# Features dealt in pairs, four more tiles turned by VectorE, and a new order of the whole program

## The chip, the cores and the metric

The kernel runs on one core of a Trainium2 chip. The metric is the device time of one execution in microseconds (us); less is better. Of TensorE (PE), VectorE (DVE), ScalarE (ACT), GpSimd (POOL) and SyncE (SP), the first four compute and SP issues the DMA transfers.

## The reference

x has 4 rows of 1024 positions with 512 features, the condition 256 features for each row, W 1536 x 512. For each row, relu of (x, the mean of x over the positions, the condition twice) times W plus b is added to x. All is float32:

```python
hidden = jnp.concatenate([cond_512, cond_512], axis=-1)
x_mean = jnp.mean(x, axis=1, keepdims=True)
fused = jnp.concatenate([x, x_mean * ones_L, hidden[:, None, :] * ones_L], axis=-1)
relation = jax.nn.relu(jnp.einsum('bld,do->blo', fused, W) + b)
return x + relation
```

The mean and the condition are the same at every position of a row, so their part of the product is one bias vector per row.

## The kernel before

The 4096 positions are cut into 32 tiles of 128 positions; a tile is multiplied by the first 512 rows of W. TensorE wants the features on the partitions, so every tile has to be turned first. The 512 features are dealt to four groups j = 0 to 3 of 128 features: feature 4a + j stands on partition a of group j. W is loaded to match (line 120).

Both x and W are split into a high part (rounded to the multiplier's format) and a low part (the rest). The task `h` makes x's high part on ScalarE, and sums over the positions beside it; `l` makes the low part on VectorE or GpSimd; `wh` and `wl` do the same for W. A tile and a group take three products on TensorE (line 348): high by high, low by high, high by low. That is 12 products of 128x512 for each tile, or 24 of half the width for the last one, t = 31, which is finished in two halves.

Tiles are turned in two ways, by units (`UNITS`). Units 0 to 3 (tiles 0; 1; 2 and 3; 4 to 7) are turned by TensorE: a 128x128 transpose for each tile and group that reads every fourth float of x's rows (task `T`, line 244). The others, four tiles each, are loaded a second time as `z` in 512-byte pieces, one DMA for each block of 32 partitions (task `Z`, four for each unit, three buffers), and VectorE turns 32x32 blocks of them (`T`, line 246), into PSUM for j = 0 and 2 and into SBUF for j = 1 and 3:

```python
zs[z_of(u)][:, : n * NQ].rearrange("p n (a j) -> p n j a", j=J)[:, :, j]
```

The bias of a row comes from the sums (`to`), W's second part (`M`, `m`, line 302), the third part and the condition (`V`, `ac`, `g`, `d`), a fold, a product with ones (`pb`, line 326) and a copy (`bc`). Products go to five PSUM banks. Tiles 0 to 11 (way K) are copied out (`K`), get the bias (`b`, GpSimd, line 419), a relu (`r`, ScalarE, line 427) and are added to x (`F`, GpSimd, line 431). Tiles 12 to 17 (way B) get the bias while they are copied out. The rest (way I) find the bias in the bank (`P`) and one VectorE operation does relu and addition (`F`, line 406). `S` stores a tile. `X` loads x for TensorE's turning and for the final addition; the x of tiles 4 to 7 stays in SBUF from the start to their addition.

Nothing is scheduled when the program is built: `ORDER`, a list of task names, is walked once, and each engine and SP's DMA queue get their instructions in that order. `@d`, `@a` and `@p` name the engine where a task has a choice. Each engine works its list in order. `fill` is a product on zeros that nobody reads.

Of the kernel before, what the change touches and what calls it, by code (L numbers as in the profile page):

```python
# [27 lines left out]
p1.3.2 l2.3@d p0.3.2 l2.2@d p1.2.1 T3.1 T3.3 h3.1 T3.0 ac0@p T3.2 K0@a l3.1@d Z5.0 Z5.1 p2.3 h3.0 t0 h3.3 p2.1
ac1@p g0.0 l3.3@d p3.0 l3.0@d d0.0 p1.3.1 p3.3 Z6.2 Z6.3 K1@a p2.2 h3.2 p5.0 g0.1 l3.2@d g1.0 p3.1 d0.1 T4.0
Z6.0 Z6.1 p6.1 T4.3 p6.3 d1.0 as0 h4.0 p4.1 T4.1 to0 p3.2 g2.0 m0.0 p2.0 K3@a m0.1 p5.2 h4.3 T4.2 p4.3 g1.1  # L30
h4.1 p5.1 d1.1 m0.2 Z7.0 Z7.1 K2@a p5.3 m0.3 h4.2 Z7.2 Z7.3 p6.0 l4.3@p l4.0@d f0 p7.3 l4.2@d g2.1 l4.1@p p6.2
fa0 p4.2 vh0 d2.0 K5@a T5.1 p4.0 p8.2 vl0 h5.1 p7.1 T5.3 K6@a l5.1@p p8.1 T5.0 h5.3 p8.0 d2.1 K4@a pb0 T5.2
# [20 lines left out]
def kernel(  # L53
# [123 lines left out]
    for part, (j0, n) in enumerate([(0, 2), (2, 2)]):  # L177
        @task(f"W{part}")
        def _(e, j0=j0, n=n):
            dma(e, out=xs[W_SLOT][:, j0 : j0 + n], in_=Wv[0, :, j0 : j0 + n])  # L180
    for h in range(2):
        @task("M" + "ab"[h])
        def _(e, h=h):
            dma(e, out=w_mean[:, 2 * h : 2 * h + 2], in_=Wv[1, :, 2 * h : 2 * h + 2])
# [38 lines left out]

    for u, (t0, n) in enumerate(UNITS):
        r = t0 // NK
        s = row_units[r].index(u)
        for j in range(J):
            buf, col = place[u, j]
            m = n * P
            if n == 1:  # L230
                xT = ps_x[u % 2][:, j * m : (j + 1) * m]
            elif n == 2:
                xT = (ps_o[4], acc)[j // 2][:, j % 2 * m : (j % 2 + 1) * m]
            elif u in BY_PE:
                xT = (*ps_x, ps_o[4], acc)[j]
# [234 lines left out]
```

## Time and profile before

| | us |
|---|---|
| median of 3 runs | 104.17 |
| lowest and highest | 103.57, 104.91 |
| span of the profiled execution (the only time that its page gives) | 104.4 |
| PE busy | 97.5 |
| DVE, ACT, POOL busy | 71.4, 62.2, 71.8 |

The span runs from the first to the last instruction of the profiled execution. A busy share is an average over the span; what a stage is worth is read from that stage's rows. In a row of instructions the first number is the start from the span's beginning, the second the length, and the brackets tell how long the engine was idle before it and what ended that. Matmuls overlap, so the distance between their starts, not their length, is what one costs. "px", "po" and "acc" are PSUM banks, "z" and "x" the two loads of x.

### The profile page before, as it was taken

The numbers are of one execution on the slowest core, as the hardware profiler recorded it, in microseconds if no ns is written. First come the engines' busy times: TensorE is split into PE (matmuls) and PEld (weight loads), VectorE is DVE, ScalarE is ACT, GpSimd is POOL, SyncE is SP. The second block draws the span as 40 slices with busy tenths as digits, with TensorE's granted clock in tenths as the row PEclk, the third lists the DMA queues.
The fourth block names the chain that finished last, engine by engine and source line by source line (L and its number), as shares of the span: only waits on it lengthen the run. The fifth ranks groups of instructions, "written<-read, shape, count | busy, mean of one in ns | idle before, by whom it ended". The sixth has DMA issues, their size and how long they took to land.

```text
span 104.4 us, 1435 instructions
## 1 busy us (share of the span) xinstructions
PE 97.5 (93%) x441; PEld 77.9 (75%) x441; DVE 71.4 (68%) x111; ACT 62.2 (60%) x154; POOL 71.8 (69%) x72
## 2 busy tenths in 40 slices
PE   6959999999978899999999999999999999999980
PEld 2347898888846588888888887887878888888870
DVE  1094946292899999999999999998968400622060
ACT  5248447879157785789984796899449502313000
POOL 4060609892970989996989999959999899904000
PEclk9999999999999999999999999999999999999999
...
GB/s 53 308 350 383 419 251 216 318 213 193 195 215 212 192 164 217 233 223 313 163 15 221 324 279 398 404 205 232 150 0 230 371 209 218 385 402 400 396 297 116
DMA packets 22657, 26.31 MB, mean 252 GB/s; under 512 B 1269, under 2 KB 13817, under 8 KB 22650
## 3 DMA queue, kind: packets, MB, share of 16 engines
...
q8 instruction: 3, 0.05, 0.2%
q14 instruction: 4, 0.03, 0.1%
...
## 4 chain that ended last, share of the span: by engine, by line
PE 77%; DVE 8%; DMA 6%; ACT 4%; issue 1%; POOL 1%; SPq 1%; POOLq 0%; DVEq 0%
PE po L348 73%; DMA x<-in_x_dram 6%; DVE acc L302 2%; DVE xT L246 2%; ACT hi L252 2%; ACT o L415 2%; PE acc L244 1%; DVE px L246 1%; PE po L244 1%; PE px L244 1%; PE acc L326 1%; DVE lo L258 1%; DVE v_acc L322 1%; DVE acc L314 1%; ACT term L280 1%
## 5 line engine op out<-in xcount | busy, mean ns | idle before, releaser
L348 PE MATMUL po<-w_hi,lo 128*128 128x512 f32 (+1 forms) x132 | 50.8, 386 | 1.2 <-DVE lo L258 1.2
L348 PE MATMUL po<-w_hi,hi 128*128 128x512 f32 (+1 forms) x132 | 50.8, 387 | 1.0 <-ACT w_hi L215 0.7
L348 PE MATMUL po<-w_lo,hi 128*128 128x512 f32 (+1 forms) x132 | 50.1, 385 | 0.0
L348 PEld LDWEIGHTS po<-w_hi,hi 128*128 128x128 f32 x132 | 24.8, 188 | 6.9 <-ACT w_hi L215 1.2
L348 PEld LDWEIGHTS po<-w_hi,lo 128*128 128x128 f32 x132 | 24.9, 188 | 6.3 <-DVE lo L258 1.6
L348 PEld LDWEIGHTS po<-w_lo,hi 128*128 128x128 f32 x132 | 24.8, 188 | 4.8
L431 POOL TENSOR_TENSOR x<-o,x 128x512 f32<-128x512 f32 x18 | 23.0, 1295 | 4.6 <-ACT o L427 4.6
L406 DVE SCALAR_TENSOR_TENSOR x<-po,x 128x512 f32<-128x512 f32 x13 | 8.8, 688 | 15.5 <-PE po L348 12.1
L258 POOL TENSOR_TENSOR lo<-xT,hi 128x512 fp32r<-128x512 f32 x12 | 15.5, 1297 | 3.7 <-ACT hi L252 3.6
L252 ACT ACTIVATE hi<-px 128x512 fp32r<-128x512 f32 (+1 forms) x22 | 10.4, 477 | 10.0 <-PE px L244 6.6
L258 DVE TENSOR_TENSOR lo<-px,hi 128x512 fp32r<-128x512 f32 (+1 forms) x22 | 11.4, 539 | 6.8 <-ACT hi L252 6.7
L419 POOL TENSOR_TENSOR o<-o,bias 128x512 f32<-128x512 f32 x12 | 15.3, 1294 | 0.0
L302 DVE SCALAR_TENSOR_TENSOR acc<-w_mean,tot,acc 128x512 f32<-128x512 f32 x16 | 11.9, 746 | 3.0 <-ACT o L415 2.5
L246 DVE STREAM_TRANSPOSE px<-z 128x512 f32<-128x512 f32 x12 | 13.0, 1100 | 0.9 <-DMA z<-in_x_dram 0.9
L427 ACT ACTIVATE o<-o 128x512 f32<-128x512 f32 x18 | 10.6, 620 | 4.9 <-POOL o L419 4.9
L246 DVE STREAM_TRANSPOSE xT<-z 128x512 f32<-128x512 f32 x12 | 13.0, 1086 | 0.0
L402 ACT ACTIVATE po<-bias 128x512 f32<-128x512 f32 x13 | 7.6, 592 | 3.5 <-DVE x L406 2.2
L252 ACT ACTIVATE hi<-xT 128x512 fp32r<-128x512 f32 x12 | 7.5, 624 | 1.2 <-DVE xT L246 1.2
L221 POOL TENSOR_TENSOR w_lo<-x,w_hi 128x256 fp32r<-128x256 f32 (+1 forms) x3 | 3.2, 1080 | 7.2 <-DVE w_hi L217 3.8
L415 ACT ACTIVATE o<-po 128x512 f32<-128x512 f32 x12 | 6.9, 586 | 0.8 <-PE po L348 0.8
L284 POOL TENSOR_TENSOR cond<-cond,term 128x512 f32<-128x512 f32 x4 | 5.2, 1293 | 2.6 <-ACT term L280 2.6
L280 ACT ACTIVATE term<-wc,cT 128x512 f32<-128x512 f32 x8 | 5.6, 715 | 0.4 <-POOL wc L274 0.4
...
## 6 DMA issues: line engine op xcount, KB each, us to landing
...
x<-in_L_cond_W_dram SPq DMA_DIRECT2D x1, 1024.0 KB, 10.6
w_mean<-in_L_cond_W_dram SPq DMA_DIRECT2D x2, 512.0 KB, 10.2
...
```

The lines of the kernel that those rows point to most:

```text
L246: nc.vector.transpose(xT.rearrange("p (n t) -> p n t", t=Q), zs[z_of(u)][:, : n * NQ].rearrange("p n (a j) -> p n j a", j=J)[:, :, j])
L252: nc.scalar.activation(his[buf][:, col : col + m], xT, AF.Copy, accum_out=sums[:, r, j, s : s + 1])
L258: nc_of[e].tensor_tensor(los[buf][:, col : col + m], xT, his[buf][:, col : col + m].bitcast(F32), ALU.subtract)
L280: nc.scalar.activation(terms[k], wc[:, k], AF.Copy, scale=cT[:, k, r : r + 1])
L302: nc.vector.scalar_tensor_tensor(acc, w_mean[:, j, :], tot[:, r, j : j + 1], acc, ALU.mult, ALU.add)
L348: nc.tensor.matmul(v, lhsT=a[:, col : col + P], rhs=m, start=WAYS[t] != "I" and key not in done, stop=done.count(key) == 3 * J - 1, skip_g ...
L402: nc.scalar.activation(bank(t), biases[r], AF.Copy)
L406: nc.vector.scalar_tensor_tensor(x_tile(t), bank(t), 0.0, x_tile(t), ALU.max, ALU.add)
L415: nc.scalar.activation(o, bank(t), AF.Copy)
L419: nc_of[e].tensor_tensor(o, o, biases[r], ALU.add)
L427: nc.scalar.activation(o, o, AF.Relu)
L431: nc.gpsimd.tensor_tensor(x_tile(t), o, x_tile(t), ALU.add)
```

## The change

Features are dealt otherwise: feature 8a + 2j + e stands on partition 2a + e of group j, so a group has pairs of neighbouring features. W's first two parts are loaded for even and odd partitions apart, in rows of 2 KB: `W` in three pieces for each parity, `M` in one. VectorE's transposes read pairs of floats, 32 bytes from pair to pair, where they read single floats 16 bytes apart.

Tiles 4 to 7 leave TensorE: they become the first unit that comes through z. For tiles 0 to 3 a copy (task `y`) gathers a group's 128 features side by side, and TensorE's transposes read that; the copies use the last four of the twelve parking buffers, and the banks that these transposes write are dealt anew. The relu of a parked tile may run on VectorE, and its addition to x on VectorE or GpSimd. `ORDER` is a new list.

```diff
-    UNITS = [(0, 1), (1, 1), (2, 2), (4, 4)] + [(t, 4) for t in range(NK, NT, 4)]
-    BY_PE = (0, 1, 2, 3)
+    E = 2
+    UNITS = [(0, 1), (1, 1), (2, 2)] + [(t, 4) for t in range(4, NT, 4)]
+    BY_PE = (0, 1, 2)
+    Y_PARTS = {0: [(0, 1), (1, 1), (2, 2)], 1: [(0, 2), (2, 2)]}
+    W_PARTS = [(0, 1), (1, 1), (2, 2)]
...
-    Wv = W.rearrange("(s p j) o -> s p j o", p=P, j=J)
+    Wv = W.rearrange("(s a j e) o -> s j a e o", s=3, j=J, e=E)
...
+    for i in range(E):
+        for part, (j0, n) in enumerate(W_PARTS):
+            @task(f"W{part}.{i}")
+            def _(e, i=i, j0=j0, n=n):
+                dma(e, out=xs[W_SLOT][i::E, j0 : j0 + n], in_=Wv[0, j0 : j0 + n, :, i].rearrange("j a o -> a j o"))
+
+        @task(f"M{i}")
+        def _(e, i=i):
+            dma(e, out=w_mean[i::E], in_=Wv[1, :, :, i].rearrange("j a o -> a j o"))
...
+    def gathered(t):
+        return parks[PARKS - 1 - t]
+
+    for t in range(sum(UNITS[u][1] for u in BY_PE)):
+        for h, (j0, n) in enumerate(Y_PARTS.get(t, [(0, J)])):
+            @task(f"y{t}.{h}")
+            def _(e, t=t, j0=j0, n=n):
+                dst = gathered(t).rearrange("p (j a e) -> p j a e", j=J, e=E)[:, j0 : j0 + n]
+                src = x_tile(t).rearrange("p (a j e) -> p j a e", j=J, e=E)[:, j0 : j0 + n]
+                if e == "a":
+                    nc.scalar.activation(dst, src, AF.Copy)
+                else:
+                    nc_of[e].tensor_copy(dst, src)
...
-                        v = x_tile(t0 + i).rearrange("p (f j) -> p j f", j=J)[:, j]
+                        v = gathered(t0 + i)[:, j * P : (j + 1) * P]
...
-                    xT.rearrange("p (n t) -> p n t", t=Q), zs[z_of(u)][:, : n * NQ].rearrange("p n (a j) -> p n j a", j=J)[:, :, j]
+                    xT.rearrange("p (n t) -> p n t", t=Q),
+                    zs[z_of(u)][:, : n * NQ].rearrange("p n (a j e) -> p n j a e", j=J, e=E)[:, :, j],
...
-            nc.scalar.activation(o, o, AF.Relu)
+            if e == "d":
+                nc.vector.tensor_scalar(o, o, 0.0, None, ALU.max)
+            else:
+                nc.scalar.activation(o, o, AF.Relu)
...
-            nc.gpsimd.tensor_tensor(x_tile(t), o, x_tile(t), ALU.add)
+            if e == "g":
+                nc.vector.scalar_tensor_tensor(x_tile(t), o, 0.0, x_tile(t), ALU.max, ALU.add)
+            else:
+                nc_of[e].tensor_tensor(x_tile(t), o, x_tile(t), ALU.add)
...
-relu X0.0 W0 B X0.1 X0.2 C W1 fill fill fill fill fill fill T0.2 T0.3 X1.1 T0.0 T0.1 X1.0 h0.0 V h0.1 l0.0@d
+X0.1 X0.0 fill relu W1.0 fill W1.1 fill W0.1 fill W0.0 fill W2.1 fill y1.1@d y1.0@p W2.0 fill X0.2 y0.2@d y0.0@p
```

TensorE's list before, from its third product on, so behind tile 0's four transposes, nine fills and two products (x_65 holds x of tiles 0 to 3, po_136 and po_137 the products of tiles 0 and 1, hi_75 and lo_89 tile 0's parts, hi_76 tile 1's high part; the rows at L244 are transposes):

```order
L348 MATMUL po_136<-w_hi,hi_75 128x512
L244 MATMUL px_142<-term_123,x_65 128x128 x4
L348 MATMUL po_136<-w_hi,lo_89 128x512
L348 MATMUL po_136<-w_lo,hi_75 128x512
L244 MATMUL acc<-term_123,x_65 128x128 x2
L244 MATMUL po_140<-term_123,x_65 128x128 x4
L348 MATMUL po_137<-w_lo,hi_76 128x512 x2
```

With the change, from its first transpose on, after seven fills (o_113 and o_114 hold the gathered tiles 1 and 0, lo_90 is tile 1's low part; the rows at L262 are transposes):

```order
L262 MATMUL acc<-term_123,o_113 128x128 x2
L262 MATMUL px_142<-term_123,o_114 128x128
L262 MATMUL po_140<-term_123,o_114 128x128 x2
L262 MATMUL po_139<-term_123,o_113 128x128
L262 MATMUL px_141<-term_123,o_114 128x128
L262 MATMUL po_139<-term_123,o_113 128x128
L367 MATMUL po_136<-w_hi,hi_75 128x512
L367 MATMUL po_137<-w_hi,hi_76 128x512
L367 MATMUL po_136<-w_hi,lo_89 128x512
L367 MATMUL po_137<-w_hi,lo_90 128x512 x2
```

All eight transposes of tiles 0 and 1 now stand ahead of the first product, and the products of the two tiles alternate; before, the transposes of the first tiles stand between products.

VectorE's list around its first transposes before (z_69 is the first z buffer, here tiles 8 to 11; lo_94 and the others are low parts of tiles 4 to 7):

```order
L258 TENSOR_TENSOR lo_94<-px_142,hi_80 128x512
L266 STREAM_TRANSPOSE cT<-bias_118 32x64
L258 TENSOR_TENSOR lo_96<-acc,hi_82 128x512
L258 TENSOR_TENSOR lo_93<-px_141,hi_79 128x512
L258 TENSOR_TENSOR lo_95<-po_140,hi_81 128x512
L246 STREAM_TRANSPOSE px_141<-z_69 128x512
L246 STREAM_TRANSPOSE xT_121<-z_69 128x512
L246 STREAM_TRANSPOSE xT_120<-z_69 128x512
```

And with the change, where z_69 holds tiles 4 to 7 and lo_91, lo_92 are low parts of tiles 2 and 3:

```order
L277 TENSOR_TENSOR lo_91<-px_141,hi_77 128x256
L285 STREAM_TRANSPOSE cT<-bias_118 32x64
L277 TENSOR_TENSOR lo_92<-px_142,hi_78 128x256 x2
L264 STREAM_TRANSPOSE xT_120<-z_69 128x512
L264 STREAM_TRANSPOSE px_142<-z_69 128x512
L264 STREAM_TRANSPOSE xT_121<-z_69 128x512
L264 STREAM_TRANSPOSE px_141<-z_69 128x512
L432 COPY o_103<-po_136 128x512
L277 TENSOR_TENSOR lo_96<-xT_121,hi_82 128x512
```

Four transposes of tiles 4 to 7 now stand where low parts of these tiles stood, and the low parts follow them.

SP's queue begins like this before (x_63 receives W's first part, x_64 its third, x_66 x of tiles 4 to 7):

```order
L145 DMA x_65<-in_x_dram 128x512
L145 DMA x_63<-in_L_cond_W_dram 128x1024
L145 DMA b_sb<-in_L_cond_b_dram 1x512
L145 DMA x_65<-in_x_dram 128x512
L145 DMA x_65<-in_x_dram 128x2x512
L145 DMA bias_118<-in_cond_dram 4x256
L145 DMA x_63<-in_L_cond_W_dram 128x1024
L145 DMA x_66<-in_x_dram 128x2x512 x2
L145 DMA x_64<-in_L_cond_W_dram 128x2x1024
L145 DMA z_69<-in_x_dram 32x16x128 x4
L145 DMA w_mean<-in_L_cond_W_dram 128x1024 x2
```

And with the change:

```order
L148 DMA x_65<-in_x_dram 128x512 x2
L148 DMA x_63<-in_L_cond_W_dram 64x512 x4
L148 DMA x_63<-in_L_cond_W_dram 64x2x512 x2
L148 DMA x_65<-in_x_dram 128x2x512
L148 DMA bias_118<-in_cond_dram 4x256
L148 DMA z_69<-in_x_dram 32x16x128 x4
L148 DMA x_64<-in_L_cond_W_dram 128x2x1024
L148 DMA z_70<-in_x_dram 32x16x128 x2
L148 DMA b_sb<-in_L_cond_b_dram 1x512
L148 DMA z_70<-in_x_dram 32x16x128 x2
```

W's six pieces stand ahead of the x of tiles 2 and 3, z's first unit follows directly, and x_66 has moved to the twenties of the list.

## Rows read from the trace of the kernel before

**Rows 1.** The page: busy time, TensorE's clock in 40 slices, the last chain by line.

```profile
PE 97.5 (93%) x441; PEld 77.9 (75%) x441; DVE 71.4 (68%) x111; ACT 62.2 (60%) x154; POOL 71.8 (69%) x72
...
PEclk9999999999999999999999999999999999999999
...
PE po L348 73%; DMA x<-in_x_dram 6%; DVE acc L302 2%; DVE xT L246 2%; ACT hi L252 2%; ACT o L415 2%; PE acc L244 1%; DVE px L246 1%; PE po L244 1%; PE px L244 1%; PE acc L326 1%; DVE lo L258 1%; DVE v_acc L322 1%; DVE acc L314 1%; ACT term L280 1%
```

**Rows 2.** The chain that ended last, a piece: start, length, what.

```profile
2.52 6.01 DMA x<-in_x_dram
```

**Rows 3.** Timeline of PE at the start: start, length, instruction.

```profile
3.71 0.74 PE L244 MATMUL px<-term,x 128*128 128x128 f32 x4
...
5.78 0.47 PE L348 MATMUL po<-w_hi,hi 128*128 128x512 f32 x1 [0.69 <-ACT w_hi L215]
...
13.78 0.63 PE L244 MATMUL px<-term,x 128*128 128x128 f32 x4
14.25 0.65 PE L244 MATMUL acc<-term,x 128*128 128x128 f32 x4
...
15.62 0.48 PE L348 MATMUL po<-w_hi,hi 128*128 128x512 f32 x1
```

**Rows 4.** Timeline of PE: two waits, and sixteen products on end.

```profile
31.78 0.51 PE L348 MATMUL po<-w_hi,lo 128*128 128x512 f32 x1 [1.15 <-DVE lo L258]
...
36.50 0.51 PE L348 MATMUL po<-w_hi,hi 128*128 128x512 f32 x1 [0.30 <-ACT o L415]
...
95.63 0.39 PE L348 MATMUL po<-w_hi,hi 128*128 128x512 f32 x1
...
99.26 0.39 PE L348 MATMUL po<-w_hi,lo 128*128 128x512 f32 x1
```

**Rows 5.** Windows: length, busy us of each engine, clock, DMA share, GB/s.

```profile
30.24:36.84 6.60, 5.14 (x21) 3.60 (x20) 6.54 (x9) 5.03 (x12) 3.01 (x4) 1.00 1.17 198
36.84:68.40 31.56, 31.56 (x140) 25.97 (x139) 31.33 (x42) 25.50 (x61) 30.06 (x28) 1.00 0.95 248
68.40:101.34 32.94, 32.90 (x156) 27.15 (x154) 16.14 (x25) 13.94 (x29) 22.67 (x20) 1.00 0.73 267
101.34:104.40 3.06, 0.00 (x0) 0.00 (x0) 0.42 (x1) 0.00 (x0) 0.00 (x0) 1.00 0.41 151
```

**Rows 6.** Windows of the start.

```profile
4.10:5.60 1.50, 1.00 (x7) 0.37 (x5) 0.46 (x3) 0.99 (x6) 0.00 (x0) 1.00 0.85 197
5.60:8.60 3.00, 2.17 (x10) 1.29 (x10) 2.25 (x6) 1.28 (x9) 1.61 (x2) 1.00 1.02 375
```

**Rows 7.** Timeline of ACT, SP and DVE at the start.

```profile
5.24 0.72 ACT L215 ACTIVATE w_hi<-x 128x256 fp32r<-128x256 f32 x2
...
5.95 6.57 SPq L145 DMA_DIRECT2D z<-in_x_dram  x4
...
9.89 0.42 DVE L217 CAST w_hi<-x 128x512 fp32r<-128x512 f32 x1
```

**Rows 8.** Groups by line and shape: count, busy us, mean ns, idle before.

```profile
L246 DVE STREAM_TRANSPOSE xT<-z 128x512 f32<-128x512 f32 x12 | 13.0, 1086 | 0.0
...
L258 DVE TENSOR_TENSOR lo<-px,hi 128x512 fp32r<-128x512 f32 x14 | 9.2, 683 | 1.4 <-ACT hi L252 1.4
...
L217 DVE CAST w_hi<-x 128x512 fp32r<-128x512 f32 x1 | 0.4, 418 | 0.0
...
L252 ACT ACTIVATE hi<-xT 128x512 fp32r<-128x512 f32 x12 | 7.5, 624 | 1.2 <-DVE xT L246 1.2
...
L258 POOL TENSOR_TENSOR lo<-xT,hi 128x512 fp32r<-128x512 f32 x12 | 15.5, 1297 | 3.7 <-ACT hi L252 3.6
```

**Rows 9.** Timeline of POOL and DVE: first work on V, first on z.

```profile
15.87 2.54 POOL L274 TENSOR_TENSOR wc<-x 128x512 f32<-128x512 f32 x2 [3.61 <-DMA z<-in_x_dram]
...
21.02 1.12 DVE L246 STREAM_TRANSPOSE px<-z 128x512 f32<-128x512 f32 x1 [0.91 <-DMA z<-in_x_dram]
```

**Rows 10.** The tile z: from issue of a transfer to its landing.

```profile
DMA to landing us min/median/max: 5.4/8.1/12.4
```

More of the change, by code (lines that the diff above doesn't have):

```diff
@@ L28 @@
[L28 to L32, printed above, removed]
@@ L48 @@
-F29 p31.1l S30 p31.3l p31.2l S29 F31l S31l
+X0.1 X0.0 fill relu W1.0 fill W1.1 fill W0.1 fill W0.0 fill W2.1 fill y1.1@d y1.0@p W2.0 fill X0.2 y0.2@d y0.0@p
+y0.1@a T1.0 T1.1 C T0.1 T0.2 h1.1 T0.3 wh1@d Z3.1 T1.2 h0.1 T0.0 T1.3 l1.1@d h1.0 p0.1.0 Z3.0 wl1@p l0.1@d wh0r@a
+p1.1.0 l1.0@d Z3.3 p0.1.1 wh0l@d h0.2 p1.1.1 h0.0 l0.2@d Z3.2 p1.0.1 h0.3 l0.0@d p1.0.0 h1.2 wl0r@p p0.0.0 wh3@d
+h1.3 p0.1.2 wh2@a p1.1.2 l1.2@d V wl0l@d p0.0.1 p0.3.0 wl3@d Z4.3 p1.3.0 p1.0.2 y3.0@p y2.0@a p0.0.2 l1.3@d p0.2.0
@@ new lines @@
+Z4.2 l0.3@d p1.2.1 wl2@d p1.3.1 p0.2.1 p1.2.0 T2.0 B T2.1 T2.2 Z4.1 h2.0 T2.3 p0.3.1 l2.0@d h2.2 p0.3.2 p0.2.2 t3
+Z4.0 h2.1 p3.0 h2.3 l2.1@d t1 p2.0 l2.2@d l2.3@d p2.1 T3.1 p3.2 T3.2 p2.3 h3.1 T3.3 p1.3.2 l3.1@p p3.3 T3.0 h3.3 M1
+p2.2 K0@d M0 h3.0 p1.2.2 l3.3@d h3.2 p4.1 Z5.2 K1@a l3.0@d p5.1 to0 K2@a l3.2@d p5.3 Z5.0 ac1@p ac0@d p6.0 t2 t0
+Z5.3 p7.3 g0.1 p6.1 g0.0 Z5.1 p5.0 d0.0 p5.2 T4.1 p7.0 T4.0 d0.1 g1.0 T4.3 p3.1 K5@a Z6.0 T4.2 p6.2 d1.0 as0 p6.3
+h4.1 m0.0 Z6.2 h4.3 p4.3 l4.1@p m0.1 g1.1 p7.2 m0.2 Z6.3 K3@a l4.3@p p4.2 m0.3 g2.0 p10.1 Z6.1 h4.0 d2.0 p8.1 f0
@@ new lines @@
+l4.0@d K6@a Z7.0 p7.1 fa0 d1.1 p4.0 vh0 Z7.2 h4.2 p8.3 vl0 g2.1 p8.0 T5.3 K4@a d2.1 l4.2@d p11.0 T5.2 pb0 p11.3
+bc0@a T5.1 h5.3 p11.2 b1@p T5.0 as1 p8.2 Z8.1 h5.1 p9.2 Z7.3 l5.3@p h5.0 l5.1@d Z7.1 p10.2 Z8.0 h5.2 l5.0@d p9.0
+K7@a l5.2@d to1 Z8.3 K8@a p9.1 b2@p T6.3 r1@a p9.3 T6.1 Z8.2 p12.3 b0@p T6.0 K9@a h6.3 p10.0 T6.2 h6.1 p12.2 m1.0
+l6.3@p Z9.1 h6.0 m1.1 p13.3 X1.0 h6.2 Z9.2 b5@p m1.2 p11.1 r0@a m1.3 p10.3 X3.1 K11@a F0@p l6.2@d p13.0 f1 l6.0@d
+K10@a X1.1 p12.1 Z9.3 g3.0 l6.1@p T7.0 p16.2 fa1 Z9.0 p14.0 b6@p T7.3 vh1 p14.3 T7.1 h7.3 p15.1 vl1 h7.0 p12.0 T7.2
@@ new lines @@
+h7.1 p16.3 l7.3@d h7.2 l7.1@p pb1 T8.3 p14.2 bc1@a to2 as2 p15.3 K12 b4@p p15.2 m2.0 p16.1 m2.1 F1@p r4@a p13.2 m2.2
+r2@a p17.1 m2.3 F2@p S1 X4.1 T8.1 p14.1 f2 p13.1 fa2 h8.1 F4@p S2 X5.0 p16.0 vh2 K13 S0 r5@a p17.3 S4 vl2 X5.1 F5@p
+p17.0 l7.2@d K14 pb2 p17.2 bc2@a l8.1@p T8.2 S5 P18 p15.0 X2.0 l7.0@d X3.0 P19 p18.2 d3.0 K16 X4.0 h8.2 p19.0 T9.1
+X2.1 g3.1 p19.1 b3@p T8.0 r12@a K17 p18.1 P21 h8.0 d3.1 p19.3 h8.3 l8.0@d X7.0 p19.2 h9.1 l8.2@d l8.3@p p18.0 P22
+T9.2 p18.3 r3@a T9.0 h9.2 p21.3 F3@p T9.3 h9.0 p21.2 F19 h9.3 p22.3 K15 S19 as3 to3 S3 p22.1 F18 r16@a l9.1@p p22.2
@@ new lines @@
+m3.0 P20 r6@a m3.1 p22.0 F16@p P23 m3.2 p20.0 m3.3 p21.0 b10@p b7@d p20.2 f3 X6.1 fa3 p20.3 b9@p F22 p23.3 vh3 r15@a
+l9.3@p vl3 p20.1 S22 r14@a p23.2 p21.1 pb3 F21 p23.0 bc3@a F14@d P24 p23.1 P27 p24.0 F23 r13@a p24.1 F20 P26 S23
+p27.2 X6.0 P28 l9.2@d S20 r7@a p27.1 S16 r17@a F7@d S21 p26.1 P25 F6@d p24.2 r9@a l9.0@d S6 p27.3 F9@p b8@d p26.3
+F15@d F12@p p27.0 p25.1 F27 b11@p p26.0 S27 p24.3 S14 S7 p28.1 S18 F24 S9 p25.3 r8@d P29 F13@d F8@p p28.3 P31r r10@a
+F17@d S13 p26.2 r11@a S12 p25.2 X7.1 F26 F11@p S24 p31.0r F10@d S15 p28.0 S26 p31.1r S17 p28.2 p25.0 F28 p29.3 F25
@@ L49 @@
+S28 p29.0 S10 P30 S25 p29.1 P31l S11 p31.2r p31.3r p30.3 F31r S31r p30.0 S8 p29.2 p30.1 F29 p30.2 S29 p31.0l F30
+p31.2l p31.3l S30 p31.1l F31l S31l
 """.split()
@@ L176, in _ @@
                 dma(e, out=z[i * Q : (i + 1) * Q, : n * NQ], in_=zv[r, i, :, k0 * NQ : (k0 + n) * NQ, :])
[L177 to L184, printed above, removed]
+    for i in range(E):
[6 more added lines that the diff above has]
+            dma(e, out=w_mean[i::E], in_=Wv[1, :, :, i].rearrange("j a o -> a j o"))
     @task("V")
@@ L229 @@
             m = n * P
[L230 to L235, printed above, removed]
+            if u == 0:
+                xT = ((ps_x[0], ps_x[1], ps_o[4], ps_o[4])[j])[:, j % 2 * m : (j % 2 + 1) * m]
+            elif u == 1:
+                xT = (acc, ps_o[3])[j // 2][:, j % 2 * m : (j % 2 + 1) * m]
+            elif u == 2:
+                xT = ps_x[j // 2][:, j % 2 * m : (j % 2 + 1) * m]
             else:
@@ L426, in _ @@
         def _(e, o=o):
-            nc.scalar.activation(o, o, AF.Relu)
+            if e == "d":
+                nc.vector.tensor_scalar(o, o, 0.0, None, ALU.max)
+            else:
+                nc.scalar.activation(o, o, AF.Relu)
         @task(f"F{t}")
         def _(e, t=t, o=o):
-            nc.gpsimd.tensor_tensor(x_tile(t), o, x_tile(t), ALU.add)
-        @task(f"G{t}")
-        def _(e, t=t, o=o):
-            nc.vector.scalar_tensor_tensor(x_tile(t), o, 0.0, x_tile(t), ALU.max, ALU.add)
+            if e == "g":
+                nc.vector.scalar_tensor_tensor(x_tile(t), o, 0.0, x_tile(t), ALU.max, ALU.add)
+            else:
+                nc_of[e].tensor_tensor(x_tile(t), o, x_tile(t), ALU.add)
     for name in ORDER:
```

19 lines of the change are left out of this document (removed).

## The prediction

> **What bounds the kernel now.** I read the page first. TensorE is busy for 97.5 us of a span of 104.4, at granted clock 1.00 in every slice, and the chain that ended last runs through the products of line 348 for 73% of the span [rows 1]. VectorE, ScalarE and GpSimd are busy for 60 to 69%. So the question is when TensorE's list starts, how long it is, and how often it waits. That needs TensorE's rows in order of time.
>
> The list's length: sixteen products take 99.26 - 95.63 = 3.63 us, 0.227 each; a product of half the width I count at half of that; four 128x128 transposes take 14.25 - 13.78 = 0.47, or 0.118 each [rows 3, 4]. Behind the first product at 5.78 stand 372 whole products (84.4), 24 halves (2.7), 28 of the 32 transposes (3.3) and four bias products (0.9): 91.3 us. The last half product ends at 101.34, 95.56 after the first began. TensorE therefore loses 4.3 us. 1.3 of them fall before 15.62, where 23 products (5.2) and 28 transposes (3.3) take 9.84 us: there it waits for loads of x and for W's high part [rows 3]. About 2.0 fall in two waits, at 31.78 for a low part from VectorE (1.4 with its restart) and at 36.50 for a bank (0.6) [rows 4]. From 36.84 to 68.40 it is busy 31.56 of 31.56 us and from 68.40 to 101.34 for 32.90 of 32.94 [rows 5]. So some 1.0 is left for everything else. Behind the list stand 3.06 us: the last vector operation and the last store [rows 5]. There is little to gain late; what can go is a start, 16 transposes and two waits.
>
> **The change part by part.** Sums are made against the profiled span, 104.4 us; the median of the runs shown is 104.17, so the span stands 0.2 above it and within their 103.57 to 104.91. A measurement of this kernel can tell about 2%: 102.1 and 106.3 us.
>
> *Transposes off TensorE.* Tiles 4 to 7 come through z and VectorE: 16 x 0.118 = 1.9 us leave TensorE's list. It is the bound there, so this counts in full.
>
> *The start.* Its new order is eight transposes, ten products before any needs group j=3 of W, 19 in all, then tiles 2 and 3. The queue's first two entries are now tiles 1 and 0. The first entry was there by 3.71, where tile 0's transposes began, and the 512 KB of W behind it by 5.24, where its cast began: some 1.6 us, or 0.8 per 256 KB [rows 3, 7]. So tile 1 lands at 3.6, tile 0 at 4.4, W's j=1 at 5.2, j=0 at 6.0, j=2 and 3 at 7.6. The gathering copies are not in the trace. GpSimd's copy of half a tile I bound by half of VectorE's cast of a whole one (0.21) and by GpSimd's own operation on a whole one (1.30), and take 0.8; VectorE's half tile lies between 0.21 and its two-input 0.68, I take 0.4 [rows 8]. Tile 1 is gathered at 4.4, tile 0 at 4.9, and the eight transposes end near 5.4, before W's j=1 is cast (0.42 behind 5.2). The first product starts at 5.7 (bounds 5.4 and 6.5), as before, though eight transposes are done by then instead of four. Nineteen products and about 0.3 of waiting for W end at 10.3. The x of tiles 2 and 3 is the ninth transfer: before, the same number of bytes (2.1 MB) had landed by 9.89, where W's second half is cast, and 1.6 MB at 2.52 + 6.01 = 8.53 [rows 2, 7]; I take 9.3. Then GpSimd gathers tile 3: between 0.42, a cast on VectorE, and twice 1.30, I take 1.3, its price for other work on 128x512 [rows 8]. The transposes run from 10.6 to 11.6, and four more products bring TensorE at 12.5 to where it stood at 15.62: 3.1 us earlier. 1.9 of that are the transposes above, 1.2 the rest.
>
> *The first tiles through z.* This is the added wait. p4.1 follows 26 products behind 11.6, at 17.5, and needs T3.1, h3.1 and, on GpSimd, l3.1. Behind it on TensorE stands everything else. The unit's 1 MB of z follows x, and V's 1 MB follows z. Before, GpSimd's work on V began at 15.87 and the first z unit was ready at 21.02: 5.15 us for 1 MB of z [rows 9]. So it lands between 9.3 + 5.15 = 14.5 and, if all of V's megabyte (2.7 us at the 375 GB/s seen in the start) shares ahead of it, 17.1; I take 15.8 [rows 6, 9]. With a transpose (0.68, below), 0.62 on ScalarE and 1.30 on GpSimd [rows 8] the low part is there at 18.4: TensorE waits 0.9. The bounds make that 0 to 2.2.
>
> *VectorE's transposes.* All 24 read single floats 16 bytes apart; whether they write PSUM (1.12 at 21.02) or SBUF (1.09) changes little, so the reading side or the transpose itself sets the time [rows 8, 9]. Now pairs are read, 32 bytes apart. Bounds: no gain (1.12, the longest) and the cheapest 512-element operation of VectorE, the cast (0.42). I take 0.68, the price of a two-input operation on 512 elements, which lies nearest to the middle. That is 28 x 0.68 = 19.0 instead of 24 x 1.09 = 26.1 us.
>
> The rows show 1.09 for single floats 16 bytes apart and nothing for pairs [rows 8]. The Trainium skill (SBUF — State Buffer, Door 1: The DMA port swizzle) says that this memory has lines of 16 bytes and gives its full rate only to at least two accesses in a line. By that rule the old pattern touches each line once and the new one twice, a transpose takes about half, an estimate of 0.55 us, and the sum is 100.1; by the rows alone, with the transpose unchanged, it is the first rival's 103.7. The slow 1.09 agrees with the rule.
>
> *The two waits.* At 31.78 TensorE waits for a low part that VectorE makes late: from 30.24 to 36.84 VectorE is busy 6.54 of 6.60 us [rows 4, 5]. With four transposes of a unit at 0.68 it has 1.6 us more per unit, and z of that unit is due about 22 (17.1 + 5.15), some 6 us before its first product (15 tile groups of 0.68 behind 17.5, near 28). Both waits go: 2.0 us. What is late next is nothing that I can name before 68 us.
>
> *Work moved between engines.* VectorE gets seven additions of x (0.68 each), two of bias, one of conditioning and a relu; GpSimd loses eleven operations of 1.29 (14 us) and a part of W, and gains three copies. VectorE's sum stays near 72 us (7.1 less, some 8 more). The seven additions stand behind the last transposes, in the stage where VectorE is busy only 16.14 of 32.94 us; that is their cover [rows 5]. At 1.09 per transpose the sum would be some 84, and the cover is thin before 68 us, where VectorE is busy 31.33 of 31.56. I cost this at 0; without the cover, seven additions in TensorE's way would be 4.8.
>
> *Queue and W.* SP's queue gets eight more entries, four of z and four of W (six pieces in place of two); their issue hides behind z's, which block the queue for 6.57 us per four anyway [rows 7]. x of tiles 4 to 7 moves past the loads of z's later units, so the core moves 1 MB more, some 5.15 us of it as z [rows 9]; the cover is the stage from 68.40 on, where the DMA engines are busy 0.73 of the time [rows 5]. W's rows of 2 KB are as long as x's. I cost this at 0; if the 5.15 us found no cover they would stand before the last stores in full.
>
> *Sum:* 104.4 - 1.9 - 1.2 - 2.0 + 0.9 = **100.2 us**. The end, 3.06 us, stays.
>
> **The rivals.**
>
> *The transposes stay at 1.09.* For: no row shows another pattern. Against: half of their time is unexplained by 512 elements if 0.68 buys two inputs. T3.3, T3.0 and the copy behind them are then 1.5 us later at p5.3 and p6.0, and the two waits of 2.0 return: 100.2 + 3.5 = 103.7.
>
> *A late start.* W comes in halves of 64 partitions, every second one. If they moved at the 197 GB/s of the stretch from 4.1 to 5.6 instead of 375, W's 1.05 MB takes 5.3 instead of 2.8 us: 100.2 + 2.5 = 102.7 [rows 6]. For: that slow stretch exists, beside W's transfer. Against: it holds the one-row load of b too, and that now comes later.
>
> *The first z unit decides (slower).* One mechanism: z is cut into 512-byte pieces and has replaced x loads as what TensorE needs next. If z's four transfers end where the first unit ends now, at 21.02, because the queue blocks (6.57 us to issue four) and V shares the engines, p4.1 starts at 23.6 and TensorE waits 6.1 instead of 0.9: 105.4. It decides from a landing at about 20.0 on, where the time is 104.4. For: z took 5.4 to 12.4 us from issue to landing [rows 10]. Against: before, 4 MB stood ahead of that unit, now 2.1.
>
> **How the numbers follow.** Forecast 0.66 (own range 98.8, with no wait for z and the fastest start, to 102.0); transposes unchanged 0.12; late start 0.13; first z unit late 0.09. Faster than 102.1: 0.62 of the forecast, 0.05 of the late start and 0.03 of unchanged transposes: 0.70. Slower than 106.3 needs the late unit with something else: 0.07. The rest, 0.23, is no change. The range, 98.8 to 104.0, leaves out most of the slower case and a little of the others.
>
> **What would show it.** Right: first product near 5.7; transposes of tiles 2 and 3 from 10.6 to 11.6; a wait of about 1 us near 17.5 for GpSimd's low part; rows of the vector transpose near 0.68 or less; TensorE without waits from 20 us on; its list ending near 97. Wrong: a first product after 7; transposes still at 1.09; a wait for z over 3 us; or waits in the stage from 37 to 68 us, where VectorE or a bank has become the bound.

## The result, and the profile after

The changed kernel took 110.02 us (median of 4 runs, 107.68 to 111.45) beside 104.54 for the kernel before on the same chip: a ratio of 1.0395 [1.027, 1.052]. It is slower; forecast were 100.2 us, 98.8 to 104.0. Some executions of either kernel fall into a slower state of the chip, so each ratio here is of the faster executions alone, with its 95% interval, and need not be that of the medians; where the record has no ratio, none is given. A run's time is some 1.8 us more than the span of its profile (107.68 and 105.9 here), and single executions of either kernel differ by some per cent: the profile of before that the prediction used (span 104.4) was one of its longer ones, the profile after is the shortest of its four.

The page of the changed kernel, its busy times, TensorE's clock, the main DMA queue and the chain that ended last by engine; it answers to [rows 1]:

```profile
PE 96.8 (91%) x423; PEld 75.0 (71%) x423; DVE 79.2 (75%) x130; ACT 61.8 (58%) x153; POOL 61.5 (58%) x63
...
PEclk9999999999999999999999999999999999999999
...
q1 hardware_dynamic: 25338, 27.27, 98.3%
...
PE 39%; DVE 18%; DMA 16%; SPq 12%; ACT 8%; POOL 2%; issue 2%; DVEq 0%
```

TensorE has 18 matmuls less (16 transposes and two fills) and the full clock throughout, but only 39% of the last chain is its own. The rest is mostly VectorE, transfers, and SP's queue itself: 12% of the span is SP issuing DMAs. The main queue's packets fill 98.3% of the DMA engines' time, where they filled 88.9% in the profile of before (93.4% in the run of before below). So something new sets the time, and the timelines tell where. SP's queue at the start, changed kernel:

```profile
1.63 3.80 SPq L148 DMA_DIRECT2D x<-in_L_cond_W_dram  x6
5.48 0.60 SPq L148 DMA_DIRECT2D x<-in_x_dram  x1
```

W's six pieces keep the queue for 3.80 us, 0.63 each, and the x of tiles 2 and 3 is issued only at 5.48. TensorE's start, changed kernel; it answers to [rows 3]:

```profile
5.94 0.70 PE L367 MATMUL po<-w_hi,hi 128*128 128x512 f32 x2 [0.57 <-DVE w_hi L221]
...
7.69 0.49 PE L367 MATMUL po<-w_hi,lo 128*128 128x512 f32 x1 [0.57 <-ACT w_hi L219]
...
10.13 0.70 PE L367 MATMUL po<-w_hi,hi 128*128 128x512 f32 x2 [0.73 <-DVE w_hi L221]
...
13.14 1.09 PE L262 MATMUL px<-term,o 128*128 128x128 f32 x8 [0.60 <-ACT o L238]
...
15.01 0.39 PE L367 MATMUL po<-w_hi,lo 128*128 128x512 f32 x1
```

The first product starts where it did, but two waits for W's high part follow, and the transposes of tiles 2 and 3 start at 13.14. At 15.01, 23 products and all of TensorE's transposes are done. Later waits on TensorE, changed kernel:

```profile
20.88 0.50 PE L367 MATMUL po<-w_hi,lo 128*128 128x512 f32 x1 [0.48 <-POOL lo L277]
31.88 0.50 PE L367 MATMUL po<-w_hi,lo 128*128 128x512 f32 x1 [0.51 <-POOL lo L277]
48.94 0.50 PE L367 MATMUL po<-w_hi,lo 128*128 128x512 f32 x1 [0.30 <-DVE lo L277]
61.64 0.50 PE L345 MATMUL acc<-v_acc,ones 128*128 128x512 f32 x1 [0.84 <-DVE v_acc L341]
```

Three wait for a low part, one for a row's bias. Behind them stand these rows of VectorE in the changed kernel, the first line answering to [rows 9]:

```profile
17.99 0.71 DVE L264 STREAM_TRANSPOSE xT<-z 128x512 f32<-128x512 f32 x1 [1.21 <-DMA z<-in_x_dram]
27.36 0.71 DVE L264 STREAM_TRANSPOSE xT<-z 128x512 f32<-128x512 f32 x1 [2.37 <-DMA z<-in_x_dram]
30.93 3.13 DVE L321 SCALAR_TENSOR_TENSOR acc<-w_mean,tot,acc 128x512 f32<-128x512 f32 x4 [1.06 <-DMA w_mean<-in_L_cond_W_dram]
```

The first two units of z and W's second part all arrive late; the chain holds that last transfer with 9.60 us from issue at 21.19. The way from there to TensorE is not always direct: before 31.88 ScalarE makes the second unit's high part only at 29.75, behind its own waits for the work on V, although the transpose had ended at 28.07; and before 48.94 VectorE works without a pause. Windows of the changed kernel (length, busy us of each engine, clock, DMA share, GB/s), answering to [rows 5]:

```profile
18.00:30.00 12.00, 11.52 (x51) 9.24 (x50) 9.47 (x15) 6.92 (x16) 6.60 (x8) 1.00 1.15 225
30.00:45.00 15.00, 14.38 (x62) 11.03 (x61) 12.99 (x19) 13.76 (x35) 12.77 (x13) 1.00 1.16 212
45.00:60.00 15.00, 14.70 (x66) 11.78 (x65) 14.27 (x22) 10.34 (x24) 12.28 (x12) 1.00 1.12 240
...
61.64:102.60 40.96, 40.92 (x188) 33.55 (x188) 32.91 (x47) 21.70 (x47) 23.96 (x19) 1.00 0.89 315
```

TensorE is idle for 1.40 us between 18 and 60 us, where VectorE has room too (36.73 of 42 us busy); the DMA engines are full there. From 61.64 to the end of its list, at 102.60, TensorE is busy for 40.92 of 40.96 us; a tail of 3.30 us follows. Two groups by line and shape, changed kernel, answering to [rows 8]:

```profile
L264 DVE STREAM_TRANSPOSE xT<-z 128x512 f32<-128x512 f32 x14 | 9.5, 691 | 3.6 <-DMA z<-in_x_dram 3.6
...
L456 DVE TENSOR_TENSOR x<-o,x 128x512 f32<-128x512 f32 x7 | 7.4, 1074 | 0.7 <-ACT o L449 0.7
```

VectorE's transposes fell from 1.09 to 0.69 us. The additions given to VectorE cost 1.07 each on average.

### The profile page after: what moved, and what is told of

It reads as the page before. It is cut to its first block, busy times and chain, and to the rows that moved or that the text cites. A ratio compares the mean times of both kernels' runs of the same rounds, so it can differ in the third digit from the quotient of the medians.

```text
span 105.9 us, 1419 instructions
## 1 busy us (share of the span) xinstructions
PE 96.8 (91%) x423; PEld 75.0 (71%) x423; DVE 79.2 (75%) x130; ACT 61.8 (58%) x153; POOL 61.5 (58%) x63
## 2 busy tenths in 40 slices
DMA packets 25345, 27.36 MB, mean 258 GB/s; under 512 B 1397, under 2 KB 15993, under 8 KB 25338
## 3 DMA queue, kind: packets, MB, share of 16 engines
q1 hardware_dynamic: 25338, 27.27, 98.3%
## 4 chain that ended last, share of the span: by engine, by line
PE 39%; DVE 18%; DMA 16%; SPq 12%; ACT 8%; POOL 2%; issue 2%; DVEq 0%
PE po L367 38%; SPq L148 12%; DMA w_mean<-in_L_cond_W_dram 9%; DVE acc L321 9%; DMA x<-in_x_dram 7%; ACT hi L271 3%; DVE lo L277 3%; DVE xT L264 2%; DVE px L264 2%; POOL lo L277 2%; ACT fold L329 2%; ACT v_acc L337 2%; DVE acc L333 1%; DVE v_acc L341 1%; PE acc L345 1%
## 5 line engine op out<-in xcount | busy, mean ns | idle before, releaser
L277 POOL TENSOR_TENSOR lo<-xT,hi 128x512 fp32r<-128x512 f32 x11 | 14.8, 1346 | 9.2 <-ACT hi L271 9.1
L456 POOL TENSOR_TENSOR x<-o,x 128x512 f32<-128x512 f32 x11 | 15.4, 1409 | 7.8 <-ACT o L449 5.6
L438 POOL TENSOR_TENSOR o<-o,bias 128x512 f32<-128x512 f32 x10 | 13.8, 1392 | 0.0
L277 DVE TENSOR_TENSOR lo<-px,hi 128x512 fp32r<-128x512 f32 (+2 forms) x20 | 11.3, 587 | 2.8 <-ACT hi L271 2.8
L264 DVE STREAM_TRANSPOSE xT<-z 128x512 f32<-128x512 f32 x14 | 9.5, 691 | 3.6 <-DMA z<-in_x_dram 3.6
L271 ACT ACTIVATE hi<-xT 128x512 fp32r<-128x512 f32 x14 | 8.8, 626 | 3.8 <-DVE xT L264 3.8
L271 ACT ACTIVATE hi<-px 128x512 fp32r<-128x512 f32 (+2 forms) x20 | 10.2, 514 | 0.8 <-PE px L262 0.7
L264 DVE STREAM_TRANSPOSE px<-z 128x512 f32<-128x512 f32 x14 | 9.7, 701 | 0.1
L456 DVE TENSOR_TENSOR x<-o,x 128x512 f32<-128x512 f32 x7 | 7.4, 1074 | 0.7 <-ACT o L449 0.7
L303 POOL TENSOR_TENSOR cond<-b_sb,term 128x512 f32<-128x512 f32 x4 | 5.2, 1305 | 2.6 <-ACT term L299 2.6
```

What stands on the lines that cost most here:

```text
L264: nc.vector.transpose(xT.rearrange("p (n t) -> p n t", t=Q), zs[z_of(u)][:, : n * NQ].rearrange("p n (a j e) -> p n j a e", j=J, e=E)[:, : ...
L271: nc.scalar.activation(his[buf][:, col : col + m], xT, AF.Copy, accum_out=sums[:, r, j, s : s + 1])
L277: nc_of[e].tensor_tensor(los[buf][:, col : col + m], xT, his[buf][:, col : col + m].bitcast(F32), ALU.subtract)
L438: nc_of[e].tensor_tensor(o, o, biases[r], ALU.add)
L456: nc_of[e].tensor_tensor(x_tile(t), o, x_tile(t), ALU.add)
```

## The experiments

The diffs show, of a line of `ORDER`, only the piece that changes.

### The kernel before, once more

No edit.

> The kernel before once more, for a profile with its own time beside it: all theories expect a span of 101.5 to 102.5 us with some 1.8 us around it, TensorE's list beginning near 5.8 and ending near 99, so that the span of 104.4 that the prediction was made against was one of the longer executions.

It took 103.08 us, span 101.3, and is one of the shorter executions of this kernel. SP's queue at the start of this run, TensorE's rows, and windows:

```profile
1.16 0.42 SPq L145 DMA_DIRECT2D x<-in_L_cond_W_dram  x1
...
2.13 0.82 SPq L145 DMA_DIRECT2D x<-in_x_dram  x2
```

```profile
5.95 0.50 PE L348 MATMUL po<-w_hi,hi 128*128 128x512 f32 x1 [0.90 <-ACT w_hi L215]
...
15.00 0.48 PE L348 MATMUL po<-w_hi,hi 128*128 128x512 f32 x1
```

```profile
18.00:30.00 12.00, 12.00 (x54) 9.93 (x54) 10.32 (x13) 9.61 (x22) 9.25 (x10) 1.00 1.17 247
30.00:45.00 15.00, 15.00 (x68) 12.43 (x67) 14.87 (x20) 12.16 (x31) 13.60 (x13) 1.00 1.20 208
45.00:60.00 15.00, 15.00 (x68) 12.39 (x67) 14.83 (x20) 12.04 (x27) 13.90 (x14) 1.00 0.99 247
...
98.27:101.30 3.03, 0.00 (x0) 0.00 (x0) 0.42 (x1) 0.00 (x0) 0.00 (x0) 1.00 0.41 150
```

The two waits of [rows 4] are absent: TensorE is busy for 42 of 42 us between 18 and 60. And the point that stood at 15.62 stands at 15.00, as in the changed kernel at 15.01, although that has 16 transposes less to do by then. So in these two profiles, each among the shortest of its kernel, the change's start gains nothing, and the whole difference comes later: 105.9 - 101.3 = 4.6 us, of which 4.3 lie between 15.0 and the list's end and 0.3 in the tail.

### W in six pieces, and on two queues

The kernel before with nothing but W's first part cut into six pieces of 64 partitions, as in the changed one (its second part is in halves by parity too), and the old deal of features:

```diff
-relu X0.0 W0 B X0.1 X0.2 C W1
+relu X0.0 W0.0 W0.1 W1.0 W1.1 B X0.1 X0.2 C W2.0 W2.1
```

> The kernel before, with W's first part loaded in six pieces of 64 partitions and its second in two, the old deal of features kept. Theory start: the x of tiles 2 and 3 is issued some 1.5 us later and lands at 10 to 11 instead of 8.53; the time grows by 1 to 2 us (ratio 1.01 to 1.02). Theory pieces: the same or more. Theory order or z: no change, ratio 0.995 to 1.005.

Measured: 108.17 us (106.67 to 108.65), ratio 1.0264 [1.0136, 1.0392]. SP's queue and TensorE's waits in this run:

```profile
1.15 2.45 SPq L146 DMA_DIRECT2D x<-in_L_cond_W_dram  x4
...
4.17 0.83 SPq L146 DMA_DIRECT2D x<-in_x_dram  x2
```

```profile
7.83 0.75 PE L246 MATMUL px<-term,x 128*128 128x128 f32 x4 [0.25 <-DMA x<-in_x_dram]
...
34.14 0.50 PE L350 MATMUL po<-w_hi,lo 128*128 128x512 f32 x1 [1.38 <-DVE lo L260]
```

In the run of before above, x of tile 1 is issued at 2.13 and these transposes start at 6.75. Cutting W costs by itself. The two waits of [rows 4] are here again, at 34.14 and, 0.31 for a bank, at 38.83. Here VectorE waits 2.11 us for W's second part before its sums at 28.93. So of the three profiles with the old deal and eight tiles turned by TensorE, two have these waits, and only the shortest has not.

The other way round: the changed kernel, with three of W's pieces on ScalarE's queue, ahead of its first activation.

```diff
-X0.1 X0.0 fill relu W1.0 fill W1.1 fill W0.1 fill W0.0 fill W2.1 fill y1.1@d y1.0@p W2.0 fill
+X0.1 X0.0 fill W1.0 W1.1@a fill W0.1 W0.0@a fill W2.1 W2.0@a relu fill fill fill y1.1@d y1.0@p fill
```

> The changed kernel, with three of W's six pieces issued by ScalarE's queue instead of SP's. Theory start (SP spends some 0.6 us on each of six small pieces, so x of tiles 2 and 3 is issued at 5.48 and lands at 12.4): that x is issued near 3.6 and lands near 10.8, the transposes of tiles 2 and 3 begin near 11.5 instead of 13.14, the span falls by 1.2 to 1.9 us below 105.9. Theory pieces (64 partitions of 2 KB rows move slowly whoever issues them): the transposes begin at 13.14 within 0.4 and the span stays. Theory order (only the new list's chains matter later): the start moves, the end of TensorE's list does not.

Measured: 105.4 us (103.96 to 107.34, 10 runs), ratio 1.0105 [1.0054, 1.0157]. That takes back 2.9 of the 4.0 points. SP's queue, TensorE and GpSimd (the copy of tile 3) in this run, whose profiled execution is the longest of the ten:

```profile
1.62 1.92 SPq L148 DMA_DIRECT2D x<-in_L_cond_W_dram  x3
4.34 0.40 SPq L148 DMA_DIRECT2D x<-in_x_dram  x1
```

```profile
12.07 1.09 PE L262 MATMUL px<-term,o 128*128 128x128 f32 x8 [0.36 <-ACT o L238]
```

```profile
11.36 0.66 POOL L240 COPY o<-x 128x512 f32<-128x512 f32 x1 [2.91 <-DMA x<-in_x_dram]
```

W's last piece lands at 7.30 instead of 9.47: the same bytes in the same pieces arrive earlier when two queues issue them, at 379 GB/s from 3.6 to 7.5 us, where one queue brought 233. So for W the issue was the limit, not the rate of 64-partition transfers. For the x of tiles 2 and 3 it was so only in part. Issued 1.14 us earlier, it lands only 1.09 us earlier, 6.97 us after its issue, because z follows it directly; in a run below with W on two queues and another x in z's place it is issued at 4.21 and lands at 8.83. The waits behind 19 us stay much as they are, and so do some 1.0 points.

### Tiles 4 to 7 through z, or back on TensorE

The kernel before with tiles 4 to 7 through z, in 16-byte steps, and their x loaded late; W and the deal are the old ones.

```diff
-    BY_PE = (0, 1, 2, 3)
+    BY_PE = (0, 1, 2)
...
-T0.2 T0.3 X1.1 T0.0 T0.1 X1.0 h0.0 V
+T0.2 T0.3 Z3.0 Z3.1 T0.0 T0.1 Z3.2 Z3.3 h0.0 V
```

> The kernel before, with tiles 4 to 7 through z and VectorE, the old deal kept, their x loaded later. Theory z (the DMA engines are full to 60 us, and 1 MB in 512-byte pieces takes 5 us where x took 2.6): TensorE's list is 1.9 us shorter, but it waits 3 to 6 us more before 40 us, and the time grows by 1 to 4 us (ratio 1.01 to 1.04). Theory order (the new list alone costs the time): the time falls by up to 1.9 us, ratio 0.98 to 1.00.

Measured: 110.27 us (107.72 to 111.77), ratio 1.0379 [1.0241, 1.0516]: 16 transposes less on TensorE, and slower. TensorE's waits in this run, and the window behind them:

```profile
18.58 0.49 PE L348 MATMUL po<-w_hi,hi 128*128 128x512 f32 x1 [1.43 <-ACT hi L252]
21.74 0.60 PE L348 MATMUL po<-w_hi,lo 128*128 128x512 f32 x1 [2.67 <-DVE lo L258]
22.14 0.63 PE L348 MATMUL po<-w_lo,hi 128*128 128x512 f32 x1
22.56 0.63 PE L348 MATMUL po<-w_hi,hi 128*128 128x512 f32 x1
```

```profile
22.00:25.00 3.00, 3.00 (x8) 2.32 (x8) 2.73 (x4) 2.12 (x6) 2.91 (x4) 0.50 1.05 339
```

What came last here is VectorE, not a transfer: from 17 to 22 us it is busy for 5.00 of 5.00 us, with transposes of 1.0 us each and a low part that took 1.59 at 19.50. So this run does not tell the price of z's megabyte from that of the slow transposes. The wait costs twice: after it TensorE's granted clock is 0.50, its level of 1.2 GHz, for 3 us, and products stand 0.42 apart instead of 0.23.

Then the changed kernel with tiles 4 to 7 gathered and turned by TensorE again, their x loaded early, and one of their low parts moved from GpSimd to VectorE; everything else is left:

```diff
-    BY_PE = (0, 1, 2)
+    BY_PE = (0, 1, 2, 3)
...
-T1.0 T1.1 C T0.1 T0.2 h1.1 T0.3 wh1@d Z3.1
+T1.0 T1.1 C T0.1 T0.2 h1.1 T0.3 wh1@d X1.0
...
+y4.0@p y5.0@a y6.0@d y7.0@p
```

> The changed kernel, with tiles 4 to 7 gathered and turned by TensorE again and their x loaded early; the rest of its order stays. Theory z: TensorE's list grows by 1.9 us, its waits between 13 and 62 us shrink by 3 to 4, the span falls to 103.5 to 105, ratio near 1.02. Theory start alone or theory order: the waits stay and the span grows to 107 to 108.

Measured: 107.08 us (106.95 to 107.18), ratio 1.0253 [1.0166, 1.0339]. Its windows, and its only wait over 0.2 us behind 11 us:

```profile
14.00:30.00 16.00, 16.00 (x79) 13.13 (x78) 9.48 (x20) 8.99 (x23) 6.76 (x8) 1.00 1.16 248
30.00:60.00 30.00, 29.97 (x131) 24.11 (x130) 27.72 (x41) 24.72 (x61) 25.72 (x24) 1.00 0.85 168
```

```profile
60.80 0.50 PE L347 MATMUL acc<-v_acc,ones 128*128 128x512 f32 x1 [0.83 <-DVE v_acc L343]
```

With 1 MB of z less the DMA share from 30 to 60 falls to 0.85, and the waits at 20, 31, 37 and 49 us are gone. Taking tiles off TensorE saved 1.9 us and cost 2.4 in waits: behind 15 us the changed kernel loses 4.6 us against its products' price of 0.227 each, this one 2.2. The net 0.5 us is most of the 0.7 between the two profiles (105.9 and 105.2); the two ratios' intervals overlap. The wait for the bias at 61 is the new order's own.

### The new deal alone, and other combinations

The order of before with the deal in pairs, all eight tiles gathered, W in four pieces on SP's queue (`[(0, 2), (2, 2)]` by parity), then the same with half of W on ScalarE's queue:

```diff
-T1.3 T1.0 T1.2
+y1.0@p T1.3 T1.0 T1.2
```

> The kernel before and its order, with features dealt in pairs alone: W's first part in four pieces on SP's queue, all eight tiles that TensorE turns gathered first, no tile moved to z. Theory pairs are worth it (VectorE's transposes 0.69 instead of 1.09, so TensorE's two waits between 30 and 37 us go): the gain of 1.5 to 2 us against 1 to 1.5 us for W's two extra issues and the gathering, ratio 0.99 to 1.005. Theory that the gathering stands on TensorE's path: ratio 1.01 to 1.03.

> The same with two of W's four pieces on ScalarE's queue. Theory start: 1 to 1.5 us less than on one queue, ratio 0.98 to 0.995; that would beat both kernels. Theory gathering: the same as on one queue within half a per cent.

Measured: 106.28 us (106.15 to 106.91), ratio 1.0238 [1.0154, 1.0322], and 107.54 us (106.97 to 109.18), ratio 1.0329 [1.0226, 1.0431]. VectorE's busy time falls to 63.3 us from 71.6 in the run of before, and the time does not fall with it. In neither run does TensorE wait behind 17 us, as in the shortest run of before, so whether the faster transposes took away the two waits of [rows 4] stays open. The gathering copy is now between a load and a transpose. TensorE at the start of the first of the two:

```profile
8.62 0.66 PE L260 MATMUL px<-term,o 128*128 128x128 f32 x4 [1.44 <-POOL o L238]
```

The new deal alone is no better with two queues, nor is the kernel with tiles 4 to 7 back on TensorE when W goes on two queues:

> Both undone at once: tiles 4 to 7 back on TensorE, and three of W's six pieces on ScalarE's queue. Theory two causes (W's issue costs some 2.9%, z some 1.4%, one behind the other): ratio 0.990 to 1.003. Theory one cause (both only hide the same late transfers): ratio 1.005 to 1.015, as with the two queues alone. Theory order (the new list itself costs a per cent): above 1.005 as well, with TensorE's waits after 20 us unchanged.

Measured: 107.08 us (105.55 to 108.71), where the kernel before took 104.45 on the same chip. If the two causes were all, this would have come level with before, and it did not. GpSimd's copy of tile 3 in this run:

```profile
8.88 0.66 POOL L240 COPY o<-x 128x512 f32<-128x512 f32 x1 [0.65 <-DMA x<-in_x_dram]
```

The x of tiles 2 and 3 is there 2.4 us earlier than with z behind it (11.36 above), but TensorE's transposes of it start only at 12.51. In this profile and in that of the new deal on two queues TensorE's first products stand 0.43 apart, from 6.5 to 9.6 us and from 6.75 to 13.8, as at the lower level of 1.2 GHz. The windows read 1.00 there, but the trace's record of the granted clock begins only at 9.86 and 13.68; in the other twelve profiles it begins between 3.6 and 6.5. In both a copy of tile 0 or W's cast is late, with W's other half on the second queue. That the two queues compete for the DMA engines then is possible and was not shown, so what two queues bring is known only for the changed kernel's own order. The wait for the bias is here too (0.83 at 60.48), as in the run on one queue.

### The changed kernel once more, the mean earlier, the additions back

Four kernels on one chip: the changed kernel without an edit; with `to2` ahead of a low part on GpSimd and `pb0` behind one more tile's products; that with W on two queues; and with nine operations of VectorE (seven `F`, two `b`) back on GpSimd.

```diff
-T5.2 pb0 p11.3
+T5.2 p11.3 pb0
...
-h7.2 l7.1@p pb1 T8.3 p14.2 bc1@a to2
+h7.2 to2 l7.1@p pb1 T8.3 p14.2 bc1@a
```

> The changed kernel once more, as what the next three stand beside on the same chip. All theories: ratio 1.03 to 1.05 against the kernel before; a profile shows the waits for z's low parts near 20 and 31 us and for the mean near 61, and in a longer execution these waits are longer, not the rest of the list.

> The changed kernel with three tasks moved: row 2's sum ahead of a low part on GpSimd's list (it stood behind one that took 1.81 us beside VectorE's), and the first bias product one tile group later on TensorE. Theory chain (the wait of 0.84 at 61.64 and 0.27 at 36.81 hang on the place of these tasks): TensorE's list ends 1.0 to 1.5 us earlier, ratio about 0.012 below the changed kernel's. Rival (what is late there is z, whatever the order): the wait at 61.64 stays within 0.3 and the time with it.

> That and three of W's six pieces on ScalarE's queue, behind its table load so that tile 0's x keeps its place. Theory start: the transposes of tiles 2 and 3 begin near 11.7 instead of 13.14 and the first product stays near 6.0; with the chain the time falls by 2.5 to 4 us below the changed kernel's, ratio 0.995 to 1.01. If start and chain only pass the wait on to z, ratio 1.02 or more.

> The changed kernel with the seven additions to x and the two of bias back on GpSimd, where they take 1.30 instead of the 1.07 and 1.39 that they took on VectorE. Theory off the path (TensorE is busy 40.92 of 40.96 us from 61.64 on): the end of TensorE's list stays within 0.3 us, the time within half a per cent, unless GpSimd's backlog comes out behind the list as a longer tail. Rival (the two engines' sharing costs the time): the time falls by 1 us or more.

| | median us (lowest, highest) | ratio |
|---|---|---|
| changed kernel again | 110.04 (107.51, 111.5) | 1.032 [1.0189, 1.0451] |
| mean earlier | 108.01 (107.07, 110.07) | 1.0268 [1.0177, 1.0358] |
| mean earlier, W on two queues | 106.04 (104.31, 108.57) | 1.0019 [0.9952, 1.0086] |
| additions on GpSimd | 111.22 (109.42, 113.05) | none |

The changed kernel was profiled here in an execution of 111.5 us, which shows the longest wait for W. TensorE's rows there:

```profile
12.24 0.70 PE L367 MATMUL po<-w_hi,hi 128*128 128x512 f32 x2 [2.87 <-DVE w_hi L221]
...
15.73 1.36 PE L262 MATMUL px<-term,o 128*128 128x128 f32 x8
```

And the windows around them:

```profile
9.40:12.20 2.80, 0.00 (x0) 0.00 (x0) 0.53 (x2) 0.54 (x1) 0.00 (x0) 1.00 1.05 182
...
14.00:16.50 2.50, 2.50 (x10) 2.00 (x9) 0.23 (x1) 0.68 (x1) 0.66 (x1) 0.52 1.21 218
```

The products with W's last pieces start 2.1 us later than in the first profile, after a stretch at 182 GB/s, and the granted clock falls to 0.52 behind the wait, as after the wait in the kernel with z alone; the transposes of tiles 2 and 3 are 2.6 us later. Why W moves more slowly here stays open.

Making the mean earlier halves the wait for the bias (0.41 instead of 0.84), but a wait of 0.53 for a low part stands at 39.06, and TensorE's list does not end earlier (103.0, and 102.6 in the first profile of the changed kernel). The ratios' intervals overlap, so its worth is not settled; with both edits the kernel is level with before. No version tried is faster than before. The additions on GpSimd gain nothing: from the wait for the bias to the end of TensorE's list it takes 40.9 us as with them on VectorE, and the tail behind the list is 4.8 us instead of 3.5. VectorE's seven additions are not what costs.

## Why the prediction was wrong

Its span for the changed kernel was 100.2 us; 105.9 was measured. By its own steps:

**The base.** "1.3 of them fall before 15.62" and "About 2.0 fall in two waits" were read from a single, long execution. In the run of before above the point at 15.62 is reached at 15.00, and there is no such wait. That run is a short one, and the waits are back with W cut alone; how often they come stays open. The forecast also set a span against times: its 100.2 stands for 102.0 us, two per cent under the median of before, and not four. The chance of faster was too high from this alone.

**Transposes off TensorE: 1.9.** Right as a count (423 matmuls instead of 441), and paid for elsewhere: the kernel of before with z alone has this saving too, and is 3.8% slower, there for VectorE's list.

**The start: 3.1 us earlier.** The step that failed first is "their issue hides behind z's". W's pieces stand ahead of everything but tiles 1 and 0, nothing hides them, and each takes 0.63 us to issue with 64 partitions, where half of W in the kernel before took 0.42 with 128. First product 5.94 (forecast 5.7), good; W's j = 2 and 3 cast at 9.56 (landing forecast at 7.6), x of tiles 2 and 3 landed at 12.40 (9.3), their transposes at 13.14 (10.6). The point forecast for 12.5 came at 15.01: 2.5 us. The sum also had no term for z, which shares the DMA engines with that x. "A late start" had the right place and the wrong cause: the pieces are slow to issue, and not to move, as two queues showed. It was given 0.13, and that its price was 2.5 too is luck, for it was worked out from a rate of transfer.

**The first tiles through z: 0.9.** The mechanism and the place hold, GpSimd's low part of the first unit. z was ready at 17.99 (forecast 15.8), but TensorE was late too, so the wait cost 0.64. The slower rival did not decide here.

**VectorE's transposes: 0.68.** Measured 0.69, where the sum took its value. The half of [rows 8] that the Trainium skill's rule would give (SBUF — State Buffer, Door 1: The DMA port swizzle; the estimate was 0.55 us) was not reached; the rule's direction, that pairs are faster than single floats, agrees with the rows. In the shortest run of before the gain could buy nothing, as TensorE does not wait there behind 15.0; what it is worth with tiles 4 to 7 on VectorE no run separates.

**Two waits gone: 2.0, and nothing late next before 68 us.** They are not there in the shortest execution of before. In the changed kernel come four waits and one small one at 36.8, 3.0 us with their restarts; with many smaller gaps, 4.6 instead of 0.2 us are lost behind 15.0. Two of the waits, at 48.94 and 61.64, are a sign that the forecast itself named for being wrong. The second unit of z, due "about 22", was there at 27.36. The step that failed is "the cover is the stage from 68.40 on": z has to land before its transposes, the last at 69.4 us, and the windows of [rows 5] up to 68.40 showed DMA shares of 1.17 and 0.95 there. A megabyte more in that stage has no cover. With it gone (tiles back on TensorE), TensorE is busy for 45.97 of 46 us from 14 to 60, where the changed kernel has 44.60.

**Work moved: 0.** The cover held (no gain with the additions on GpSimd), though the price was wrong: seven additions took 1.07 us on average instead of 0.68, for the reason below, and VectorE's busy time came to 79.2 us instead of near 72.

**Tail:** 3.30 us instead of 3.03.

With the run of before as base the steps add up: 101.3 - 2.5 (start) + 0.9 = 99.7, and + 2.5 for the start that did not come + 3.4 for waits (4.3 more than in that run, instead of 0.9) + 0.3 for the tail = 105.9. The median lies 2.3 us above that execution; of the 3.8 us between its two profiles, 2.6 are in the start, where the wait for W differs. Which part of the whole each of the two causes makes is not settled: undone one by one they give back 2.9 and 1.4 points, undone together they do not give back the whole.
